# A cross-attention block in one kernel: part of the DMA issues move to ScalarE, epsilon additions may run on GpSimd, and the written-out order is a new one

## The chip, the core and the metric

The kernel runs on one core of a Trainium2 chip. The metric is the device time in microseconds of the whole kernel. A core has TensorE (PE), VectorE (DVE), ScalarE (ACT), GpSimd (POOL) and SyncE (SP), each with an instruction queue of its own that is worked off in order, and 16 DMA engines that all issuers share.

## The reference

All tensors are float32. There are 8 sequences of 256 tokens with 512 channels, 16 heads of 32, and an MLP of width 2048. The mask is all ones.

```
x = layer_norm(hidden) * ln1_w + ln1_b
q = x @ q_w + q_b;  k = ctx @ k_w + k_b;  v = ctx @ v_w + v_b
attn = softmax(q k^T / sqrt(32));  out = (attn v) @ cproj_w + cproj_b
hidden = out + hidden
y = layer_norm(hidden) * ln2_w + ln2_b          # eps = 1e-5 in both
y = gelu_tanh(y @ fc_w + fc_b) @ proj_w + proj_b
return hidden + y
```

## The kernel before

**Groups and stages.** The 8 sequences are worked off in two groups of four (1024 tokens); names carry the group as their first digit. For each group there are the context's and the normalized input's projections (k, v, q), the attention by sequence and four heads at a time (a unit), the output projection `o` with the residual (`hid`), the second normalization (`y`), the `fc` products with gelu (`h`) and the `proj` products (`pd`). The stages of the two groups overlap: group 0's MLP runs beside group 1's attention, group 0's projection beside group 1's output projection, and group 1's MLP comes last.

**Products.** Every large product is a Strassen-Winograd form: seven products of half-size blocks in place of eight, one level for q, k, v and o, two levels in the MLP. The operands' sums and differences (names with `s`, `i` or `t`, such as `pw1s`, `z0i`, `y0t`) are made by VectorE or GpSimd; three PSUM banks X, Y and W take the seven products P1 to P7, and evictions (`take`, `plus` in `quad`) move and add them into the result: t1, t2, t3, c11, c12, c21, c22. ScalarE does part of the plain evictions, VectorE the additions out of PSUM.

**Attention.** `scores` computes a unit's scores, evicts them with the mask's bias on ScalarE (`pr`), takes maxima over blocks on VectorE (`mx`), folds them, writes them to DRAM and loads them back spread over all partitions (`md`, `mm`), subtracts them (`less`, on GpSimd or VectorE) and exponentiates on ScalarE. `attend` multiplies with v and with ones for the sums (`av`); VectorE inverts and scales (`rc`, `r`, `att`).

**The second normalization.** `layer_norm` takes two 128-token tiles at a time. VectorE does statistics and aggregate, adds epsilon, GpSimd raises to −1/2, VectorE makes the bias (`nb`), and ScalarE or VectorE normalizes. For group 0 the tiles are then turned by TensorE (`ps_y`) and evicted with weight and bias to `y`; for group 1 they are stored to DRAM (`yd`), loaded back in pieces of 32x32 (`yb`) and transposed there by VectorE.

**The ends.** `hid` is also stored to DRAM (`hd`). The projection's result is transposed on VectorE (`tr`, into `tq`), the residual is loaded back from `hd` in the same turned layout (`rq`), added (`out`), and stored (`so`). At the very end of group 1 partial results go over DRAM (`lo`, `rl`) and the last quarter by `st`.

**What sets the order.** Nothing is scheduled at run time. The program is built as a list of operations; `Order.run` then replays the table PROGRAM, 2968 words, in its order. A word is an operation's name with the engine's letter behind a colon where the operation has alternatives (V for VectorE, A ScalarE, G GpSimd, S SyncE, P TensorE). A second table, PLACES, gives each buffer its slot. Each engine executes its share in the order of the words, so an instruction that waits holds everything behind it on the same engine. All loads and stores are issued by SP, through `load` and `store`.

Of the kernel before, what the change touches and what calls it, by code (L numbers as in the profile page):

```python
# [17 lines left out]
EPS = 1e-5  # L18
# [111 lines left out]
v0_0_P5 fw0i1_1:G fw0i1_2:G turn_c0_20 v0_0_t3:A fw0i1_3:G turn_c0_30 xt0_5 kws3:V v0_1_t3:A v0_0_P3 fw0i5_2:G rows1  # L130
c0_20:A rows3 stats_x0_10 c0_30:A fw0_01_1 fw0s2:V v0_1_P3 fw1_11_0 v0_0_c12:A xt0_6 fw0s3:V xt0_4 v0_0_P2 fw0i5_4:V
fcd0_7_False fw0i7_3:V fw0i7_1:V xt0_3 c0t4:V fw0i7_2:G fw1_00_1 k0_0_P2 fw0_01_0 stats_x0_01 fw1_10_1 kws1:V
fw0i1_4:G cols v0_1_P2 kws2:V fw0i6_3:G fcd0_1_True cols~1 xt1_0 fcd0_5_False aggr_x0_01 k0_1_P7 fw0i4_3:V k0_1_t1:A
aggr_x0_10 aggr_x0_00 fw0i2_1:G stats_x0_21 k0_0_t1:A fw1_10_0 eps_x0_0 stats_x0_30 pow_x0_0 qw00 k0_1_P2 stats_x0_20
fw1_00_0 fw0i6_1:G aggr_x0_20 nb_x0_0 aggr_x0_21 qw01 fw1i4_3:G fw1i4_1:V k0_0_P6 fw0i2_3:G qw11 stats_x0_11 eps_x0_2
fw1i4_2:V aggr_x0_11 eps_x0_1 fw0i7_4:V k0_1_P6 pow_x0_1 stats_x0_31 k0_0_t2:A norm_x0_01:A k0_1_c11 pow_x0_2
fw0i5_3:V fw0i2_2:G k0_0_P5 v0_1_c11 fcd0_5_True k0_1_t2:A kws4:V fw1i4_4:G k0_0_c11 k0_0_P7 nb_x0_1 v0_0_c11
fcd1_4_True norm_x0_10:A fw0s4:V norm_x0_11:A fcd0_6_False qw10 k0_1_P5 k0_0_t3:A fw1s1:V fcd0_7_True aggr_x0_30
fw1_01_1 fw0i3_3:V k0_0_P3 aggr_x0_31 fw0i3_1:V k0_1_t3:A eps_x0_3 nb_x0_2 fw1i1_1:V pow_x0_3 v0_1_c12:A k0_1_c22
norm_x0_00:A fw1i1_3:G k0_0_c22 k0_1_P3 norm_x0_20:A nb_x0_3 fw0i2_4:V fw1i5_1:G fw1i5_3:V norm_x0_21:A fcd0_2_True  # L140
fw1i1_2:G norm_x0_31:A turn_x0_10 norm_x0_30:V xt1_1 turn_x0_00 fw0i6_2:V k0_1_c12:A fcd0_4_True k0_1_P4 x0_10:A
fw1_01_0 fw0i6_4:V fcd1_5_False k0_0_c12:V x0_00:A fcd0_6_True fw1s3:V turn_x0_31 turn_x0_21 turn_x0_11 fcd0_3_False
fw1i1_4:V x0_21:A k0_0_P4 fw1s2:V x0_11:A fcd1_1_True qws3:V fw1i6_1:G turn_x0_20 fcd1_6_False k0_1_c21 turn_x0_01
fw0i3_2:V fw1i5_2:G q0_1_P1 k0_0_c21 xt1_2 x0_01:A fcd1_7_False x0_20:A fw1i5_4:V qws1:V xt1_3 turn_x0_30 qws2:V
q0_0_P1 x0_30:A x0t1:V x0_31:A x0t2:V q0_0_P2 q0_0_t1:A fw1i6_2:V stats_x1_00 fw1i6_4:G q0_0_P6 cb1_13 q0_0_c11
fw1i2_1:G cb1_02 fw0i3_4:V fw1s4:G stats_x1_01 cb1_10 s000 q0_0_t2:A x0t3:V fcd0_3_True cb1_11 q0_0_P5 ev000_20
ev000_31 fcd1_5_True ev000_21 fw1i2_2:V ev000_01 q0_1_t1:A q0_0_P7 ev000_00 fcd1_3_False x0t4:V ev000_30 fw1i2_4:G
q0_0_t3:A ev000_11 q0_1_P2 mx000_1 ev000_10 fw1i6_3:G aggr_x1_00 q0_0_c22 fcd1_6_True qws4:G q0_1_P6 stats_x1_10
aggr_x1_01 mx000_0 q0_0_P4 fw1i2_3:V mt000 fcd1_2_True q0_1_c11 fw1i3_1:G mc000_2 mc000_1 eps_x1_0 mc000_3 stats_x1_11
cb1_12 fw1i3_2:G q0_1_t2:A q0_0_P3 q0_0_c21 pow_x1_0 aggr_x1_11 fw1i7_1:V fw1i3_4:G fw1i7_2:V s020 fw1i3_3:G  # L150
aggr_x1_10 fold000 q0_1_P5 nb_x1_0 ev020_31 fw1i7_4:G q0_0_c12:V md000 ev020_20 cb1_03 fw1i7_3:G ev020_21 cb1_00
ev020_30 ev020_01 kd0_0_11 mx020_1 s002 ev020_00 cb1_01 ev020_10 ev020_11 fcd1_3_True norm_x1_00:V q0_1_P7 ev002_20
mm000 norm_x1_01:V ev002_10 eps_x1_1 mx020_0 ev002_00 pow_x1_1 ev002_30 ev002_11 v0_0_P7 ev002_31 mt020 q0_1_t3:V
mc020_2 ev002_21 nb_x1_1 q0_1_c22 mc020_3 mc020_1 ev002_01 fold020 s022 mx002_0 md020 v0_1_P7 cb1_30 ev022_21 ev022_01
mx002_1 fcd1_7_True ev022_10 norm_x1_11:A mt002 q0_1_P4 less000_0:G ev022_11 v0_0_c22 mc002_1 mm020 cT1_10
norm_x1_10:A cb1_32 mc002_2 cb1_31 mc002_3 v0_0_P4 ev022_20 fold002 cb1_33 ev022_30 v0_1_c22 less000_1:G ev022_31
md002 ev022_00 q0_1_c21 v0_1_P4 v0_0_c21 cT1_11 exp000_0 less020_0:G s010 cb1_20 v0_1_c21 cb1_23 cT1_01 q0_1_P3
ev010_01 cb1_21 cT1_00 exp000_1 cb1_22 mx022_1 less020_1:G ev010_31 ev010_10 k1_1_P1 mx022_0 ev010_21 mm002 ev010_00
vd0_0_21 ev010_11 mt022 xd1_1 q0_1_c12:V k1_0_P1 mc022_2 c1t1:G ev010_30 mx010_0 vd0_0_11 ev010_20 exp020_0 mx010_1
# [315 lines left out]
def pool(n):  # L475
# [21 lines left out]

SERVE = {
    "cq": 0.72,
    "fw": 0.75, "kw": 0.73, "qw": 0.73, "vw": 0.73, "ow": 0.69, "pw": 0.41, "md": 0.2, "mm": 1.3, "rows": 0.15,  # L500
    "prd0_1_True": 1.36, "res": 1.6, "hid": 1.45,
}
WARM, WARM2 = 14, 14


@with_exitstack
def tile_xattn_block(
    ctx: ExitStack,
    tc: tile.TileContext,
# [23 lines left out]
    nc = tc.nc  # L533
    B, S, D = x.shape
# [949 lines left out]
```

## Time and profile before

| | |
|---|---|
| three runs | 665.8, 673.46, 664.97 us |
| profiled execution, its own time | 665.78 us |
| its span, first to last instruction | 664.0 us |
| TensorE, VectorE, ScalarE, GpSimd busy | 98%, 88%, 52%, 72% |
| bytes moved by DMA | 146.96 MB, 221 GB/s on average |

Busy times are shares of the span. A transfer's issue occupies its engine's queue but isn't counted as busy. In a view of waits a row names who waited, for what, and for how long in total; in a view of groups the number behind the tile's shape is the count, then come the busy time and the mean in ns, then the idle time of the engine ahead of these instructions and what ended it.

### The profile page before, as it was taken

What the parts mean: (1) busy time and instruction counts of PE and PEld (TensorE: products, weight loads), DVE (VectorE), ACT (ScalarE), POOL (GpSimd) and SP (SyncE); (2) the same over time, 40 slices, a digit from 0 to 9 for tenths busy, and PEclk for the clock granted to TensorE, in tenths of its full rate; (3) what the DMA queues carried; (4) which work ended last, traced back from release to release, by engine and by line L of the source; (5) the groups of instructions that cost most, each with busy time, mean ns of one, the idle gap of its engine ahead of it and who ended that gap; (6) DMA issues with size and microseconds to landing.
All of it is one profiled execution on the core that took longest, in us unless ns stands there. A gap on an engine that the chain in (4) does not pass through costs nothing.

```text
span 664.0 us, 11603 instructions
## 1 busy us (share of the span) xinstructions
PE 653.6 (98%) x3985; PEld 493.2 (74%) x3985; DVE 585.3 (88%) x947; ACT 347.6 (52%) x707; POOL 476.4 (72%) x395
## 2 busy tenths in 40 slices
PE   9999999999999999999999999999999999999997
PEld 7845454577545775787777878888888888888887
DVE  3999999989999999999999999988389888898784
ACT  2255687878999789837858993011021123740000
POOL 3764579588869978898899859686366349656670
PEclk9999999999999999999999999999999999999999
DMA  8999898789987675868564466769999998439576
GB/s 269 305 351 341 254 219 270 265 190 214 279 255 215 211 278 187 257 220 267 196 221 144 141 180 202 246 218 277 151 217 230 286 221 229 125 118 223 111 157 114
DMA packets 216539, 146.96 MB, mean 221 GB/s; under 512 B 125424, under 2 KB 176928, under 8 KB 216480
## 3 DMA queue, kind: packets, MB, share of 16 engines
q1 hardware_dynamic: 216480, 146.21, 78.3%
q8 instruction: 32, 0.52, 0.3%
q14 instruction: 27, 0.22, 0.1%
HBM read 105.67 MB, written 40.50 MB: 220 GB/s over the span
## 4 chain that ended last, share of the span: by engine, by line
PE 86%; DVE 7%; ACT 3%; DMA 2%; issue 1%; SPq 0%; POOL 0%; DVEq 0%; POOLq 0%; ACTq 0%
PE pd_X L634 14%; PE fc_X L634 13%; PE pd_W L634 7%; PE av L634 7%; PE fc_W L634 7%; PE v_X L634 4%; PE k_X L634 4%; PE q_X L634 4%; PE s L634 4%; PE fc_Y L634 3%; PE pd_Y L634 3%; PE v_W L634 2%; PE k_W L634 2%; PE q_W L634 2%; PE o_X L634 2%
## 5 line engine op out<-in xcount | busy, mean ns | idle before, releaser
L1029 POOL TENSOR_TENSOR pr<-pr,mm 128x512 f32<-128x512 f32 x82 | 109.4, 1362 | 16.0 <-DMA mm<-md 13.8
L614 ACT ACTIVATE pr<-s,cols 128x256 f32<-128x256 f32 x256 | 104.4, 480 | 20.6 <-PE s L634 16.4
L1004 DVE TRANSPOSE_TENSOR_REDUCE mx<-pr 128x32 f32<-128x1024 f32 x64 | 77.7, 1223 | 3.1 <-ACT pr L614 2.9
L1032 ACT ACTIVATE pr<-pr 128x1024 f32<-128x1024 f32 x64 | 66.9, 1063 | 25.4 <-POOL pr L1029 22.4
L1212 ACT ACTIVATE h<-h,cols 128x256 f32<-128x256 f32 x128 | 56.2, 500 | 45.4 <-DVE h L625 40.2
L625 DVE TENSOR_TENSOR h<-fc_X,h 128x512 f32<-128x512 f32 x80 | 53.4, 680 | 7.8 <-PE fc_X L634 7.4
L634 PE MATMUL av<-pr,ones 128*32 128x256 f32 x512 | 34.8, 383 | 2.4 <-ACT pr L614 1.5
L625 DVE TENSOR_TENSOR h<-fc_W,h 128x512 f32<-128x512 f32 x48 | 31.8, 676 | 3.4 <-PE fc_W L634 2.9
L1024 DVE TENSOR_TENSOR pr<-pr,mm 128x1024 f32<-128x1024 f32 x23 | 32.3, 1415 | 0.0
L623 POOL TENSOR_TENSOR z0i<-z0t,z0i 128x512 f32<-128x512 f32 x14 | 20.9, 1513 | 14.5 <-PE av L634 7.5
L1011 ACT COPY mx<-mx 32x64 f32<-32x64 f32 x96 | 23.3, 243 | 12.7 <-DVE mx L1008 8.3
L634 PEld LDWEIGHTS av<-pr,ones 128*32 128x32 f32 x512 | 14.6, 109 | 18.2 <-ACT pr L614 3.7
L625 POOL TENSOR_TENSOR h<-h,fl 128x512 f32<-128x512 f32 x9 | 11.7, 1315 | 18.5 <-DVE h L625 18.1
L1012 DVE TENSOR_REDUCE mx<-mx 32x32 f32<-32x256 f32 x32 | 18.6, 581 | 3.1 <-ACT mx L1011 3.1
L634 PE MATMUL fc_X<-y1i,fl 128*128 128x256 f32 x80 | 19.7, 379 | 0.0
L625 POOL TENSOR_TENSOR po<-po,e 128x256 f32<-128x256 f32 x10 | 8.9, 910 | 14.0 <-ACT e L606 7.2
L634 PE MATMUL pd_X<-z0i,pl 128*128 128x256 f32 x80 | 18.7, 380 | 0.0
L807 ACT ACTIVATE pl<-hid,rs_y 128x512 f32<-128x512 f32 x1 | 0.8, 813 | 31.7 <-DVE rs_y L799 31.7
L623 POOL TENSOR_TENSOR z0i<-z0t,z0t 128x512 f32<-128x512 f32 x10 | 16.5, 1666 | 1.2 <-DVE z0t L625 1.2
L606 ACT ACTIVATE e<-pd_X,cols 128x256 f32<-128x256 f32 x7 | 3.3, 468 | 26.8 <-PE pd_X L634 26.8
L625 POOL TENSOR_TENSOR tq<-tq,rq 128x512 f32<-128x512 f32 x7 | 9.2, 1320 | 10.9 <-DVE tq L1312 6.3
L634 PEld LDWEIGHTS pd_X<-z0i,pl 128*128 128x128 f32 x80 | 15.1, 190 | 2.4 <-ACT po L601 0.3
(634 smaller groups left out, 1958.0 us busy)
## 6 DMA issues: line engine op xcount, KB each, us to landing
mm<-md SPq DMA_DIRECT2D x32, 512.0 KB, 5.1
pl<-prd SPq DMA_DIRECT2D x55, 256.0 KB, 3.8
fl<-fcd SPq DMA_DIRECT2D x31, 256.0 KB, 4.7
fw<-in_L_xattn_fc_w_dram SPq DMA_DIRECT2D x16, 256.0 KB, 5.8
pw<-in_L_xattn_proj_w_dram SPq DMA_DIRECT2D x32, 128.0 KB, 3.1
hid<-in_x_dram SPq DMA_DIRECT2D x8, 512.0 KB, 7.0
hd<-hid SPq DMA_DIRECT2D x8, 512.0 KB, 5.0
rq<-hd SPq DMA_DIRECT2D x32, 128.0 KB, 5.1
```

The lines of the kernel that those rows point to most:

```text
L606: nc.scalar.activation(to(), of_(), AF.Identity, bias=bias(), scale=1.0)
L614: lambda e: nc.scalar.activation(to(), of_(), AF.Identity, bias=bias(), scale=1.0))
L623: nc.gpsimd.tensor_tensor(to()[:, ts(k, 512)], in0()[:, ts(k, 512)], in1()[:, ts(k, 512)], op)
L625: E[e].tensor_tensor(to(), in0(), in1(), op)
L634: nc.tensor.matmul(o(), l(), r(), start=first, stop=True, skip_group_check=True)
L1004: T.op(f"mx{u}_{h}", [("DVE", 1.126)], [(pr[h], None)], [(mx, [h])], lambda e, h=h: nc.vector.tensor_reduce(tile_of(mx)[:, 0:64].rearrange ...
L1011: lambda e, a=a: nc.scalar.copy(tile_of(mx)[0:32, 64 + 64 * a : 128 + 64 * a], tile_of(mx)[32 * a : 32 * a + 32, 64:128]))
L1012: T.op(f"fold{u}", [("DVE", 0.38)], [(mx, [2, 3, 4, 5])], [(mx, [6])], lambda e: nc.vector.tensor_reduce(tile_of(mx)[0:32, 320:352], tile_ ...
L1024: nc.vector.tensor_tensor(p_, p_, m_[:, :, None, :].to_broadcast([P, 2, 2, S]), ALU.subtract)
L1029: E[e].tensor_tensor(p_, p_, at(M, j)[:, None, :].to_broadcast([P, 2, S]), ALU.subtract)
L1032: lambda e, h=h: nc.scalar.activation(tile_of(pr[h]), tile_of(pr[h]), AF.Exp), table="exp")
L1212: lambda e, f=f, b=b, c=c: nc.scalar.activation(at(h[f][b], c), at(h[f][b], c), AF.Gelu_apprx_tanh, bias=col(c_fcb + f * 4 + c), scale=1.0 ...
```

## The change

First, the transfers of some kinds may be issued by ScalarE as well as by SP: residuals (`rq`), results (`so`, `st`), the y tiles (`yd`, `yb`), `hd`, and the partial results (`lo`, `rl`). The table gives ScalarE 56 of the 136 of these: 17 rq, 18 so, 9 yb, 2 yd, 2 hd, 4 lo, 3 rl and 1 st. Second, the epsilon addition may run on GpSimd: 6 of 16 do, four in the first normalization and two in the second. Third, both tables are new: the same 2968 operations in another order, with other buffer slots (897 of 1290 differ), and some sums, evictions and subtractions on another engine than before. The number of matmuls is the same.

```
+def QUEUES(name):
+    return [("SP", 0.47), ("ACT", 0.47)] if name[:2] in ("rq", "so", "yd", "yb", "hd", "lo", "rl", "st") else [("SP", 0.47)]
...
     def load(name, b, keys, to, of_, mb, src=(), lead=0.0):
         return T.op(
-            name, [("SP", 0.47)], list(src), [(b, keys)],
-            lambda e: nc.sync.dma_start(to(), of_()), serve=served(name, mb), base=2.05, lead=lead,
+            name, QUEUES(name), list(src), [(b, keys)],
+            lambda e: E[e].dma_start(to(), of_()), serve=served(name, mb), base=2.05, lead=lead,
         )
...
-            name, [("SP", 0.47)], src, [(d, keys)] if d else [],
-            lambda e: nc.sync.dma_start(to(), of_()), serve=served(name, mb), base=1.4,
+            name, QUEUES(name), src, [(d, keys)] if d else [],
+            lambda e: E[e].dma_start(to(), of_()), serve=served(name, mb), base=1.4,
...
             def fn1(e, mv=mv, rs=rs):
-                nc.vector.tensor_scalar_add(tile_of(rs)[:, 0:2], tile_of(mv)[:, 1:4:2], EPS)
-            T.op(f"eps_{tag}{g}_{h}", [("DVE", 0.06)], [(mv, None)], [(rs, None)], fn1)
+                E[e].tensor_scalar_add(tile_of(rs)[:, 0:2], tile_of(mv)[:, 1:4:2], EPS)
+            T.op(f"eps_{tag}{g}_{h}", [("DVE", 0.06), ("POOL", 0.2)], [(mv, None)], [(rs, None)], fn1, lock=True)
...
 PROGRAM = """
-cq0_00_0 cq0_00_1 cq0_01_1 cq0_11_0 cq0_11_1 rows8 cq0_01_0 vw00 turn_c0_10 vw11 turn_c0_00 mk small c0_00:A vw10
```

Lines of the changed kernel stand 7 further down than before (L625 becomes L632, L1212 becomes L1219); up to the tables they are 2 to 7 off.

The order moves in every stage. Three places follow. The first is the crossing from attention to the MLP of group 0. VectorE stood thus ahead of the first y tile (`y_00`, which the first fc product reads), with the end of the second normalization (L799 is nb) among scores (`mx`, L1004 to L1012), an inverse (`rc`, `r`) and a subtraction (L1024):

```order
L799 SCALAR_TENSOR_TENSOR rs_y_1_2680<-mv_y_1_2646,rs_y_1_2680 128x2
L1004 TENSOR_REDUCE mx_2682<-pr_1_2585 128x2x2x8
L1008 STREAM_TRANSPOSE mx_2682<-mx_2682 128x64
L799 SCALAR_TENSOR_TENSOR rs_y_0_2692<-mv_y_0_2675,rs_y_0_2692 128x2
L1004 TENSOR_REDUCE mx_2537<-pr_1_2479 128x2x2x8
L1024 TENSOR_TENSOR pr_0_2368<-pr_0_2368,mm_2559 128x1024
L1012 TENSOR_REDUCE mx_2682<-mx_2682 32x32
L1055 TENSOR_REDUCE rc_2785<-av_2703 128x8
L1057 RECIPROCAL rc_2785<-rc_2785 128x8
L1058 STREAM_TRANSPOSE r_2788<-rc_2785 128x256
L1008 STREAM_TRANSPOSE mx_2537<-mx_2537 128x64
L766 TENSOR_SCALAR y_00_2799<-ps_y_00_2758,cols 128x512
```

Now the same engine has this ahead of the same y tile, with a weight sum (`pw1s`) and the scaled attention (`att`) among it:

```order
L806 SCALAR_TENSOR_TENSOR rs_y_0_2720<-mv_y_0_2684,rs_y_0_2720 128x2
L632 TENSOR_TENSOR pw1s_2752<-pw_10_2182,pw_11_2483 128x1024
L796 BN_AGGR mv_y_2_2624<-st_y_2_2604 128x2
L1019 TENSOR_REDUCE mx_2628<-mx_2628 32x32
L800 TENSOR_SCALAR rs_y_2_2780<-mv_y_2_2624 128x2
L1062 TENSOR_REDUCE rc_2785<-av_2733 128x8
L1064 RECIPROCAL rc_2785<-rc_2785 128x8
L1065 STREAM_TRANSPOSE r_2788<-rc_2785 128x256
L1011 TENSOR_REDUCE mx_2722<-pr_0_2475 128x2x2x8
L632 TENSOR_TENSOR att_00_2811<-av_2733,r_2788 128x256
L1015 STREAM_TRANSPOSE mx_2722<-mx_2722 128x64
L773 TENSOR_SCALAR y_00_2836<-ps_y_00_2794,cols 128x512
```

The weight sum, the scaled attention and a later epsilon came in ahead of the y tile, and the subtraction went further forward; over the whole way from the last addition into `hid` to this tile there is also one more maximum (L1011) and one more 256-wide sum (`pw1i`), and one aggregate, one epsilon and one nb fewer.

TensorE had, between the turning of the first tile (`ps_y_00`) and the first fc product, one unit of attention:

```order
L721 MATMUL ps_y_00_2758<-ident,v_1_11_314 128x128
L634 MATMUL av_2767<-pr_0_2273,ones 32x256 x2
...
L634 MATMUL av_2767<-pr_1_2282,xt_0_466 32x256 x2
L634 MATMUL fc_X<-y_00_2799,ow_1913 128x256 x2
L721 MATMUL ps_y_10_2822<-ident,k_1_22_1319 128x128
```

Now two further turnings stand there too, and one more unit (`av_2755`) stands directly ahead of the first turning:

```order
L641 MATMUL av_2755<-pr_1_2278,kw_218 32x256 x2
L728 MATMUL ps_y_00_2794<-ident,xn_y_00_2778 128x128
...
L728 MATMUL ps_y_20_2800<-ident,xn_y_00_2778 128x128
...
L728 MATMUL ps_y_10_2806<-ident,fl_2_2659 128x128
L641 MATMUL av_2819<-pr_0_2362,ones 32x256 x2
...
L641 MATMUL av_2819<-pr_1_2364,v_1_11_1561 32x256 x2
L641 MATMUL fc_X<-y_00_2836,qws_781 128x256 x2
```

Two turnings and a unit moved ahead of the first fc product.

The second place is ScalarE where group 1's second normalization meets the projection of group 0. Before, it held attention tiles (`att`), gelus (L1212), and then norms (L807) and the first y tiles (L751):

```order
L1212 ACTIVATE h_31_3203<-h_31_3203,cols 128x256
L1212 ACTIVATE h_20_3137<-h_20_3137,cols 128x256
L614 ACTIVATE att_10_2979<-att_10_2979,cols 128x512
L614 ACTIVATE att_01_3069<-att_01_3069,cols 128x512
L807 ACTIVATE pl_5_4130<-hid_3_4266,rs_y_3_4423 128x512
L807 ACTIVATE fl_1_3616<-hid_3_4266,rs_y_3_4423 128x512
L807 ACTIVATE xn_y_11_4473<-hid_1_3761,rs_y_1_4458 128x512
```

Now two stores of `hid` stand among the gelus, each with a wait for the last addition into its tile:

```order
L621 ACTIVATE att_11_2958<-att_11_2958,cols 128x512 x2
L601 DMA hd_120<-hid_2_4198 128x2x512
L1219 ACTIVATE h_31_3211<-h_31_3211,cols 128x256
L1219 ACTIVATE h_21_3239<-h_21_3239,cols 128x256
L1219 ACTIVATE h_31_3211<-h_31_3211,cols 128x256
L601 DMA hd_120<-hid_0_4050 128x2x512
L1219 ACTIVATE h_20_3132<-h_20_3132,cols 128x256 x2
L814 ACTIVATE xn_y_30_4433<-hid_3_4264,rs_y_3_4417 128x512
```

Both stores moved from SP's queue into ScalarE's, ahead of three gelus and of two.

The third place is a little later on ScalarE, where the y tiles come back and results go out. Before, there were only these between the norms and the first copies out of the fc banks:

```order
L807 ACTIVATE xn_y_11_4473<-hid_0_4182,rs_y_0_4478 128x512
L606 ACTIVATE e_4548<-pd_X,cols 128x256 x2
L751 ACTIVATE y_00_4683<-y_00_4683,cols 128x512
L606 ACTIVATE e_4548<-pd_X,cols 128x256
L751 ACTIVATE y_01_4696<-y_01_4696,cols 128x512
L601 COPY h_00_4731<-fc_X 128x512
```

Now stores of results (`so`, to out_dram) stand among the evictions of the fc banks:

```order
L758 ACTIVATE y_10_4751<-y_10_4751,cols 128x512 x2
L601 DMA out_dram<-tq_3_4759 32x32x32
L601 DMA out_dram<-tq_1_4710 32x32x32
L1219 ACTIVATE h_00_4767<-h_00_4767,cols 128x256
L601 DMA out_dram<-tq_3_4759 32x32x32 x2
L601 DMA out_dram<-tq_1_4710 32x32x32
L608 COPY e_0_4936<-fc_X 128x512
```

Five stores moved from SP to a place ahead of this copy.

More of the change, by code (lines that the diff above doesn't have):

```diff
@@ L130 @@
[L130 to L159, printed above, removed]
@@ L345 @@
-so1_22 out1_01:V rq1_12 pd12_P4 so1_32 pd12_c12 tr1_01 rl11 tr1_00 so1_20 out1_00:G pd13_P7 rl10 so1_00 pd14_t1
-pd14_P6 pd13_c22 so1_02 pd12_c21 tr1_13 so1_03 so1_33 pd13_P4 pd14_t2 so1_01 tr1_10 tr1_11 out1_10:G pd14_P5 pd13_c21
-tr1_12 out1_11:V pd14_P7 z1i4_4:V so1_11 so1_13 so1_10 pd14_t3 pd14_P2 pd14_P3 pd14_c11 pd14_c22 st00 so1_12 pd14_P4
-pd14_c12 st1 pd14_c21 st01
+cq0_00_1 cq0_00_0 cq0_01_0 cq0_11_0 cq0_01_1 cq0_11_1 vw00 kw00 rows3 fw0_11_1 turn_c0_10 turn_c0_00 c0_10:A vw11
+small c0_00:A vw10 vw01 cq0_10_0 turn_c0_01 rows8 turn_c0_11 c0_01:V turn_c0_31 cq0_10_1 c0_11:V turn_c0_21 fw0_11_0
@@ new lines @@
+v0_0_t3:A stats_x0_20 fw0s4:V xt0_5 v0_0_P3 fw1_10_0 fw1_00_1 kws3:V fw0i3_3:G stats_x0_10 v0_1_P3 v0_0_c12:A qw11
+stats_x0_01 fw0i5_4:G fw1_11_0 aggr_x0_20 v0_0_c11 fw0i2_1:G kws1:V fw0i7_3:G k0_0_P2 v0_1_c12:A aggr_x0_01 aggr_x0_00
+fw0i6_1:V fcd0_1_True eps_x0_0:G kws2:V fw1_10_1 pow_x0_0 k0_0_P7 stats_x0_31 qw10 fcd0_5_True fw0i6_2:G kws4:V
+fcd0_3_False fw0i6_4:G cols k0_1_P2 cols~1 fcd0_6_False stats_x0_11 qw01 k0_0_t1:A aggr_x0_11 k0_1_t1:A stats_x0_30
+k0_1_P7 aggr_x0_31 nb_x0_0 fw0i3_1:V aggr_x0_10 fw1i4_1:V eps_x0_1:G c0t4:V pow_x0_1 k0_0_P6 aggr_x0_30 eps_x0_3:V
@@ new lines @@
+pl15_4=2 pd15_X=C0 po1_2=8 pd15_Y=C3 pd15_W=2 po1_3=36 z1i3_1=82 z1i3_2=16 z1i3_3=64 z1i3_4=40 pl13_1=39 pl13_2=45
+pl13_6=5 pl13_7=66 pl13_5=72 pl13_3=48 pl13_4=42 pd13_X=0 pd13_Y=C3 pd13_W=C0 z1i7_1=38 z1i7_2=48 z1i7_3=88 z1i7_4=6
+pl17_1=63 pl17_2=20 pl17_6=62 pl17_7=50 pl17_5=35 pl17_3=4 pl17_4=34 pd17_X=C1 e1=56 pd17_Y=C2 pd17_W=C4 rq1_2=70
+tq1_2=62 rl0=36 rl1=30 rq1_3=68 tq1_3=0 z1i4_1=34 z1i4_2=20 z1i4_3=32 z1i4_4=18 pl14_1=14 pl14_2=51 pl14_6=50 pl14_7=4
+pl14_5=24 pl14_3=39 pl14_4=77 pd14_X=C1 ot0=61 pd14_Y=C4 pd14_W=1 ot1=1
```

619 lines of the change are left out of this document (322 added, 297 removed).

## The prediction

> **What bounds the kernel now.** I read the head of the page and its chain first, then TensorE's waits, then windows around the largest of them.
>
> ```profile
> span 664.0 us, 11603 instructions
> PE 653.6 (98%) x3985; PEld 493.2 (74%) x3985; DVE 585.3 (88%) x947; ACT 347.6 (52%) x707; POOL 476.4 (72%) x395
> PE 86%; DVE 7%; ACT 3%; DMA 2%; issue 1%; SPq 0%; POOL 0%; DVEq 0%; POOLq 0%; ACTq 0%
> ```
>
> TensorE is busy 653.6 of 664.0 us. What a new order can save while it keeps the 3985 matmuls is the rest, 10.4 us. VectorE is the second limit. The waits tell where those 10.4 us are:
>
> ```profile
> PE av L634 <- ACT pr L614: 1.5, 1, 1.5
> PE first L646 <- DVE warm L641: 1.0, 1, 1.0
> PE av L634 <- ACT pr L1032: 0.8, 1, 0.8
> PE ps_y L721 <- ACT fl L807: 0.8, 1, 0.8
> PE fc_X L634 <- DVE y L766: 0.7, 1, 0.7
> PE fc_W L634 <- DVE h L625: 0.4, 1, 0.4
> PE pd_X L634 <- DVE po L853: 0.3, 1, 0.3
> PE ps_c L721 <- DMA cq<-in_ctx_dram: 0.3, 1, 0.3
> ```
>
> The columns are the total (us), the count and the longest. Only one entry names a transfer, with 0.3 us, and it is a load of the context at the start, a kind that the change leaves on SP. The 1.0 us of `first` lies before any input. At the other end stands the last addition:
>
> ```profile
> 660.61 0.42 DVE L625 TENSOR_TENSOR ot<-pd_W,ot 128x256 f32<-128x256 f32 x1 [1.36 <-PE pd_W L634]
> ```
>
> TensorE ends about there, so about 3.4 us (664.0 less 660.6) are the last addition, the last store and its landing. That leaves 10.4 − 1.0 − 3.4 = **6.0 us** in the middle. Half lies in one place, where group 0 goes from attention and the output projection to its MLP:
>
> ```profile
> 240.00:250.00 10.00, 8.48 (x94) 6.03 (x96) 9.63 (x25) 8.98 (x19) 7.47 (x8) 1.00 0.93 340
> 250.00:260.00 10.00, 8.44 (x109) 5.08 (x98) 8.62 (x17) 9.81 (x22) 9.45 (x10) 1.00 0.66 208
> 400.00:664.00 264.00, 260.27 (x1257) 229.07 (x1255) 215.40 (x338) 50.76 (x106) 163.56 (x122) 1.00 0.80 195
> ```
>
> After the length of the window come the busy times of TensorE, its weight loads, VectorE, ScalarE and GpSimd, then the granted clock (1.00 throughout), the share of the DMA engines and GB/s. The first two windows leave TensorE idle for 1.52 + 1.56 = 3.08 us. From 400 on it is idle for 3.73 us, nearly all of it the 3.4 us of the tail.
>
> **The change, part by part.** All is summed against the profiled execution, 665.78 us, which is the median of the three runs (665.8) to the tenth. Its span is 664.0; about 1.8 us lie around it.
>
> *The second queue.* 56 issues move from SP to ScalarE, nearly all after 400 us. An issue occupies its engine's queue for:
>
> ```profile
> L588 SPq DMA_DIRECT2D yb<-yd x16: 303/560/1798, 460.2 to 482.3; - x16
> L588 SPq DMA_DIRECT2D rq<-hd x32: 318/498/2142, 456.2 to 643.9; - x32
> L594 SPq DMA_DIRECT2D hd<-hid x8: 370/371/807, 238.7 to 449.5; - x8
> ```
>
> At about 0.5 us (the medians) this gives ScalarE 56 × 0.5 = 28 us. It is busy for 50.8 of the 264 us from 400 on (row above), so 213 us are free there and the 28 us lie beside other work. SP loses the same 28 us. What would be gained is a transfer that lands earlier, and no wait of TensorE from 400 on names a transfer: **0** for both. The lower bound is the loss of every middle wait (rival 1), the upper one rival 2. Where ScalarE's issue also has to wait for a store's source, what stands behind it on that engine are gelus and evictions, and behind these TensorE's operands and banks: that is rival 2.
>
> At this place a page speaks against the gain too:
>
> ```profile
> 460.00:480.00 20.00, 19.70 (x91) 17.02 (x91) 9.63 (x17) 0.47 (x1) 9.44 (x8) 1.00 1.19 167
> ```
>
> The share of the DMA engines in these 20 us, where yd, yb and rq run, is 1.19: the engines are full, and a second issuer adds none. The Trainium skill, "DMA: Bandwidth & Descriptors", section "Issuing engines are not separate DMA queues", says that transfers started by several engines run on the same 16 DMA engines, and that a second issuer saves only the time of the issuing. By it the queue's term is 0 as above; by a rule under which two queues doubled the rate it would be 0 as well, since TensorE idles only 0.30 us in that window.
>
> *The epsilon additions.* 6 of 16 go to GpSimd. On VectorE, and the nearest operation on GpSimd (the power that follows, of the same size):
>
> ```profile
> L793 DVE TENSOR_SCALAR rs_x<-mv_x x8: 146/164/175, 34.0 to 120.0; 128x2 f32<-128x2 f32 x8
> L796 POOL TENSOR_TENSOR rs_x<-rs_x,neg_half x8: 683/696/865, 34.2 to 120.3; 128x2 f32<-128x2 f32 x8
> ```
>
> VectorE is relieved of 6 × 0.16 = 1.0 us. The chain of one normalization grows by between 0 (as short as on VectorE) and 0.70 − 0.16 = 0.5 us; I take 0.5, as the nearest row. It is hidden where the normalized tile waits for other tiles of the group; uncovered it costs 0.5 once, in the crossing below. Term: 0.
>
> *The order: the crossing at 240 to 260.* The chain runs from the last addition into hid (o_0's W product) through statistics, epsilon, power, norm and turn to the first y tile, which the first fc product reads:
>
> ```profile
> 243.84 0.69 DVE L625 TENSOR_TENSOR hid<-o_W,hid 128x512 f32<-128x512 f32 x1
> 256.62 0.77 DVE L766 TENSOR_SCALAR y<-ps_y,cols 128x512 f32<-128x512 f32 x1
> 257.45 1.13 PE L634 MATMUL fc_X<-y,ow 128*128 128x256 f32 x4 [0.66 <-DVE y L766]
> 258.76 1.77 DVE L625 TENSOR_TENSOR pw1s<-pw,pw 128x1024 f32<-128x1024 f32 x1
> 259.99 1.07 PE L634 MATMUL av<-pr,ones 128*32 128x256 f32 x16
> 261.86 0.48 PE L634 MATMUL fc_Y<-y,ow 128*128 128x256 f32 x1
> ...
> 265.73 0.33 PE L721 MATMUL ps_y<-ident,k 128*128 128x128 f32 x1
> 266.22 0.60 PE L634 MATMUL fc_X<-y0i,fl 128*128 128x256 f32 x2
> ```
>
> The y tile starts 12.78 us after the hid addition starts. In the new order VectorE has other rows between the same two: one maximum of scores more, one 1024-wide weight sum (1.77 us, the row at 258.76), one 256-wide sum, one product of attention with the inverse, and one aggregate, one epsilon (now on GpSimd) and one nb row less.
>
> ```profile
> L1004 DVE TRANSPOSE_TENSOR_REDUCE mx<-pr 128x32 f32<-128x1024 f32 x64 | 77.7, 1223 | 3.1 <-ACT pr L614 2.9
> L625 DVE TENSOR_TENSOR att<-av,r 128x256 f32<-128x256 f32 x32 | 12.6, 405 | 0.2
> L625 DVE TENSOR_TENSOR fw0i<-fw0s 128x256 f32<-128x256 f32 x6 | 2.9, 492 | 0.0
> L793 DVE TENSOR_SCALAR rs_y<-mv_y 128x2 f32<-128x2 f32 x8 | 2.7, 366 | 0.8 <-ACT fl L807 0.8
> L799 DVE SCALAR_TENSOR_TENSOR rs_y<-mv_y,rs_y 128x2 f32<-128x2 f32 x8 | 2.5, 324 | 0.9 <-POOL rs_y L796 0.9
> L789 DVE BATCH_NORM_AGGREGATE mv_y<-st_y 128x2 f32<-128x6 f32 x16 | 2.3, 165 | 0.1
> ```
>
> 1.22 + 1.77 + 0.49 + 0.41 − 0.17 − 0.37 − 0.32 = 3.03 us more, if VectorE idles there as before; it idled 20 − 9.63 − 8.62 = 1.75 us in the two windows, and if the added rows fill that, y is late by 1.28 only. Against it TensorE gets work ahead of the first fc product: one more av unit (259.99 to 261.86, 1.87) and two more turns (265.73 to 266.22, 0.49 each), 2.85 us. The difference lies between 1.28 − 2.85 = −1.57 and 3.03 − 2.85 = +0.18; I take the middle, **−0.7**, which is about the 0.66 us that the first fc product waits now. What is late next is the norm behind the powers: GpSimd now does one epsilon and two powers ahead of the needed one where it did two powers, which is within the +0.5 above.
>
> *The start.* The 4x128 load of bias rows that stood ahead of a piece of the first context quarters stands behind them now; the 0.3 us of `ps_c` go: **−0.3**.
>
> *The rest of the order.* All other middle waits are 6.0 − 0.7 − 0.3 = 5.0 us. Rows are exchanged everywhere, with engines too; by my tally of the rows at their durations VectorE gets about 7.6 us more and GpSimd about 9 us less, an estimate. I take these waits as neither removed nor added, since a shuffled order of the same work on a VectorE that is busy for 91% of the two windows above gives others like them; bounds −5.0 and the same +5.0. The tail keeps its last product, addition and store: 0.
>
> **Sum: 665.78 − 0.7 − 0.3 = 664.8 us.**
>
> **The rivals.**
> 1. *The order closes the middle waits.* 665.78 − 6.0 = **659.8**, and a little less where TensorE loses small steps between rows that the view does not list. For it: half of the idle is at one crossing, which has 2.85 us more of work to cover it. Against it: VectorE gets rows there, and the longest waits (av on `pr`, 1.5 and 0.8) hang on the scores' chain over ScalarE and GpSimd, which no row shows shortened.
> 2. *ScalarE's queue holds what TensorE waits for: slower.* One place is the second store of hid, whose source is VectorE's last addition of its sequence pair; behind it on ScalarE now stand two gelus, which the projection's next product needs.
>
> ```profile
> 434.57 1.67 PE L634 MATMUL o_W<-fl,a1t 128*128 128x256 f32 x7
> 438.41 0.68 DVE L625 TENSOR_TENSOR hid<-o_W,hid 128x512 f32<-128x512 f32 x1
> 439.11 0.37 SPq L594 DMA_DIRECT2D hd<-hid  x1
> L1212 ACT ACTIVATE h<-h,cols 128x256 f32<-128x256 f32 x70 | 30.1, 498 | 44.2 <-DVE h L625 40.2 <-POOL h L625 4.0
> ```
>
> The product's eight matmuls end at about 436.5 and the addition at 439.1, 2.6 us later; with the issue (0.37) and two gelus (2 × 0.50) the operand is there 4.0 us after the product, and TensorE has 6.9 us of other products ahead of the reader, by the order. It decides when VectorE is over 2.9 us later than now at that addition. By my tally its rows there grow by up to 6.7 us, which would be a wait of 3.8: 668.6. A second place of the same kind are five stores of results ahead of the eviction of an fc bank that TensorE asks for about a product (1.89 us) later: 5 × 0.49 + 0.58 for the eviction − 1.89 = +1.1. Both: **669.7**. Beyond 2%, over 679.1, it would need about four such places at once; most are covered by ScalarE's idle 213 us.
> 3. *The queues share turns.* The weights on SP get their turn against ScalarE's transfers of many small pieces.
>
> ```profile
> fl<-fcd SPq DMA_DIRECT2D x31, 256.0 KB, 4.7
> ```
>
> If a weight block that lands in 4.7 us now takes twice that once where the fc products begin, and nothing covers it, that is 664.8 + 4.7 = **669.5**. Against it: the blocks are loaded some products ahead. The Trainium skill, on the same page, section "Queues, rings and completion order", has each DMA engine take turns between its queues packet by packet, which is the mechanism of this rival; no row here shows two queues of data (the page of before lists one, and two of instructions).
>
> **How the numbers follow.** Forecast 0.52, rival 1 0.21, rival 2 0.19, rival 3 0.08. The range runs from 659.0 (rival 1, with the small steps) to 671.0 (rivals 2 and 3 with one further issue of the slow kind, 1.80 in the row of yb, less the cover). What is left out is half of rival 2's tail and the unforeseen, under 0.2. A change of 2%, 13.3 us, is about what a measurement of this kernel can tell from no change. Faster than that, below 652.5, would take more than all that TensorE idles in the middle: 0.01. Slower: a quarter of rival 2's chance, where the places add: 0.05. Within 2%: 0.94.
>
> **What would show it.** Right: TensorE busy for about 653.6 us, waits that sum to about 5 in the middle, the fc_X wait on y gone, ScalarE with about 28 us of issuing and no TensorE wait behind it, landing times of fl near 4.7, no wait on a transfer after 400. Wrong towards rival 1: two windows around the crossing with TensorE near 10. Towards rival 2: waits of pd_X on gelus (h) or of fc products on ScalarE's evictions after 400. Towards rival 3: waits on fl or pl. I would be wrong altogether if TensorE's busy time itself moved.

## The result, and the profile after

| | before | changed |
|---|---|---|
| median of 20 runs each | 665.47 us | 672.04 us (668.98 to 675.19) |
| ratio, 95% interval | | 1.0088 (1.0067 to 1.0109) |
| profiled execution, its span | 665.78, 664.0 us | 671.07, 669.2 us |

The changed kernel is slower by 0.9%, about 5.9 us by the ratio and 6.6 us by the medians. That is less than 2% but clear of noise, and the median lies 1.0 us above the range that was given. A ratio also takes in runs with a granted clock below 0.999, which for the kernel before are about 6 us longer and make up 8 of its 31, 13 of its 34 and none of its 23 runs beside the three rounds of experiments below, so the medians stand beside the ratios. The head of the page of the changed kernel:

```profile
span 669.2 us, 11633 instructions
PE 652.7 (98%) x3985; PEld 494.4 (74%) x3985; DVE 581.3 (87%) x953; ACT 348.4 (52%) x705; POOL 452.4 (68%) x390
q1 hardware_dynamic: 168736, 138.21, 71.0%
q10 hardware_dynamic: 47744, 8.00, 7.6%
PE 68%; DVE 10%; DMA 8%; issue 5%; ACT 4%; POOL 4%; SPq 1%; ACTq 0%; POOLq 0%; DVEq 0%
```

TensorE's work is the same (652.7 us against 653.6). The second queue is there: q10 with 8.00 MB. In the chain DMA has grown from 2% to 8% and "issue" from 1% to 5%, at TensorE's expense (86% to 68%). The windows by stage say where it happened; the first four rows are of before, the other four of the changed kernel (length, then busy time of TensorE, weight loads, VectorE, ScalarE, GpSimd):

```profile
0.00:180.00 180.00, 178.74 (x1117) 109.28 (x1118) 158.17 (x272) 118.45 (x244) 122.47 (x115) 1.00 0.90 269
180.00:280.00 100.00, 95.78 (x789) 61.85 (x787) 96.61 (x164) 87.61 (x181) 87.00 (x72) 1.00 0.74 235
280.00:440.00 160.00, 158.80 (x1014) 128.07 (x1011) 154.04 (x230) 95.66 (x188) 137.86 (x108) 1.00 0.63 200
440.00:640.00 200.00, 199.70 (x927) 174.73 (x926) 163.32 (x258) 45.87 (x96) 122.27 (x98) 1.00 0.84 199
```

```profile
0.00:180.00 180.00, 178.35 (x1116) 108.89 (x1117) 155.85 (x272) 116.98 (x242) 117.12 (x118) 1.00 0.91 267
180.00:280.00 100.00, 95.92 (x806) 63.96 (x804) 96.72 (x166) 88.54 (x180) 86.94 (x70) 1.00 0.74 233
280.00:440.00 160.00, 158.28 (x1009) 129.16 (x1002) 152.20 (x239) 99.32 (x191) 116.17 (x101) 1.00 0.67 216
440.00:640.00 200.00, 194.40 (x900) 168.59 (x899) 158.32 (x243) 43.52 (x93) 117.20 (x94) 1.00 0.84 191
```

TensorE's idle time rises from 1.26 to 1.65, from 4.22 to 4.08, from 1.20 to 1.72, and from **0.30 to 5.60 us**. All but 0.8 us of the loss lies behind 440 us, where nearly all of the moved transfers are. The tail is the same to 0.1 us. TensorE's waits, the largest of the changed kernel:

```profile
PE av L641 <- ACT pr L621: 3.1, 2, 2.0
PE fc_X L641 <- ACT e L608: 2.0, 1, 2.0
PE pd_W L641 <- DVE e L632: 1.8, 2, 1.5
PE fc_W L641 <- DMA e<-fcd: 1.4, 1, 1.4
PE av L641 <- ACT pr L1039: 1.2, 1, 1.2
PE first L653 <- DVE warm L648: 1.0, 1, 1.0
```

The second, third and fourth are new and lie behind 440 us (of the third, 0.9 us stay when the queue is undone, experiment 1). The second is the place that the prediction named, five stores ahead of the copy of an fc bank. ScalarE's timeline there:

```profile
508.58 0.51 ACT L1219 ACTIVATE h<-h,cols 128x256 f32<-128x256 f32 x1 [4.63 <-DVE h L632]
508.59 5.84 ACTq L601 DMA_DIRECT2D out_dram<-tq  x3
514.48 0.59 ACT L608 COPY e<-fc_X 128x512 f32<-128x512 f32 x1 [5.38 <-DMA out_dram<-tq]
```

Three stores take 5.84 us of ScalarE's queue, and the copy behind them has a 5.38 us gap that "DMA out_dram<-tq" ends: the landing of a store. The operands of the single issues in the trace tell why. Each transfer signals its landing on a semaphore; the program has eight for all its 612 transfers (101 and 103 to 109 in the operands, 76 or 77 transfers each), given out in turn in program order whatever queue issues them: in the kernel before, SP's issues take them strictly in this turn, and in the changed kernel the issues of both queues, put together, fit one such turn. A transfer whose semaphore is still taken waits at its issue until the transfer eight places before in the program has landed:

```
start    engine  transfer         waits for, signals   landed
506.96   ScalarE out_dram<-tq     107, 107             512.30
512.32   ScalarE out_dram<-tq     107, 107             516.68
560.92   ScalarE out_dram<-tq     109, 109             566.34
566.36   SP      fl<-prd          109, 109             571.63
```

The second store starts 0.02 us behind the landing of the first. The last two rows show the same wait from one queue to the other: a weight load on SP waits for a store that ScalarE issued, and `e<-fcd`, for which TensorE waits 1.4 us at 570.6, stands next behind it on SP. So the theory under test, A (A1 in its sharper form): the two queues are coupled through eight semaphores, and each holds what stands behind it on its engine. The other theories, B to D, are named in the expectations.

### The profile page after: what moved, and what is told of

Same layout as the page of the kernel before. It is cut to its first block, busy times and chain, and to the rows that moved or that the text cites. A ratio compares the mean times of both kernels' runs of the same rounds, so it can differ in the third digit from the quotient of the medians.

```text
span 669.2 us, 11633 instructions
## 1 busy us (share of the span) xinstructions
PE 652.7 (98%) x3985; PEld 494.4 (74%) x3985; DVE 581.3 (87%) x953; ACT 348.4 (52%) x705; POOL 452.4 (68%) x390
## 4 chain that ended last, share of the span: by engine, by line
PE 68%; DVE 10%; DMA 8%; issue 5%; ACT 4%; POOL 4%; SPq 1%; ACTq 0%; POOLq 0%; DVEq 0%
PE fc_X L641 11%; PE pd_X L641 10%; PE fc_W L641 6%; PE pd_W L641 6%; PE av L641 5%; PE k_X L641 4%; PE o_X L641 3%; PE v_X L641 3%; PE s L641 3%; PE pd_Y L641 2%; PE fc_Y L641 2%; PE q_X L641 2%; PE k_W L641 2%; PE o_W L641 2%; ACT pr L621 2%
## 5 line engine op out<-in xcount | busy, mean ns | idle before, releaser
L1036 POOL TENSOR_TENSOR pr<-pr,mm 128x512 f32<-128x512 f32 x78 | 101.0, 1324 | 20.5 <-DMA mm<-md 16.0
L1219 ACT ACTIVATE h<-h,cols 128x256 f32<-128x256 f32 x128 | 56.2, 500 | 68.1 <-DVE h L632 26.6
L1011 DVE TRANSPOSE_TENSOR_REDUCE mx<-pr 128x32 f32<-128x1024 f32 x64 | 77.0, 1219 | 2.6 <-ACT pr L621 2.4
L632 DVE TENSOR_TENSOR h<-fc_X,h 128x512 f32<-128x512 f32 x80 | 53.2, 679 | 10.8 <-PE fc_X L641 10.3
L632 DVE TENSOR_TENSOR h<-fc_W,h 128x512 f32<-128x512 f32 x48 | 32.3, 679 | 6.4 <-PE fc_W L641 5.8
L632 POOL TENSOR_TENSOR h<-h,fl 128x512 f32<-128x512 f32 x8 | 11.6, 1454 | 16.1 <-DVE h L632 16.1
L641 PE MATMUL pd_W<-z0i,pl 128*128 128x256 f32 x80 | 18.9, 381 | 1.8 <-DVE e L632 1.5
L613 ACT ACTIVATE e<-pd_X,cols 128x256 f32<-128x256 f32 x4 | 1.9, 474 | 33.8 <-PE pd_X L641 33.8
L630 POOL TENSOR_TENSOR z0i<-h,h 128x512 f32<-128x512 f32 x8 | 12.1, 1528 | 10.9 <-DVE po L632 10.2
L641 PEld LDWEIGHTS pd_W<-z0i,pl 128*128 128x128 f32 x80 | 15.0, 190 | 4.5 <-issue 2.6
L632 DVE TENSOR_TENSOR h<-fc_Y,h 128x512 f32<-128x512 f32 x24 | 16.3, 678 | 2.0 <-PE fc_Y L641 1.9
L632 POOL TENSOR_TENSOR tq<-tq,rq 128x512 f32<-128x512 f32 x8 | 10.8, 1354 | 9.8 <-DVE tq L1319 9.6
L630 POOL TENSOR_TENSOR z0t<-h,h 128x512 f32<-128x512 f32 x10 | 14.6, 1474 | 4.2 <-issue 4.2
L630 POOL TENSOR_TENSOR z1t<-h,z1t 128x512 f32<-128x512 f32 x6 | 9.6, 1612 | 11.6 <-PE pd_X L641 11.6
L630 POOL TENSOR_TENSOR z1i<-h,h 128x512 f32<-128x512 f32 x8 | 11.3, 1440 | 7.7 <-PE pd_X L641 7.7
```

The source lines that it names most:

```text
L613: nc.scalar.activation(to(), of_(), AF.Identity, bias=bias(), scale=1.0)
L630: nc.gpsimd.tensor_tensor(to()[:, ts(k, 512)], in0()[:, ts(k, 512)], in1()[:, ts(k, 512)], op)
L632: E[e].tensor_tensor(to(), in0(), in1(), op)
L641: nc.tensor.matmul(o(), l(), r(), start=first, stop=True, skip_group_check=True)
L1011: T.op(f"mx{u}_{h}", [("DVE", 1.126)], [(pr[h], None)], [(mx, [h])], lambda e, h=h: nc.vector.tensor_reduce(tile_of(mx)[:, 0:64].rearrange ...
L1036: E[e].tensor_tensor(p_, p_, at(M, j)[:, None, :].to_broadcast([P, 2, S]), ALU.subtract)
```

## The experiments

All were run beside the kernel before on the same chip (7, 9 and 11 on another chip than the others); ratios are to that, and where it matters its median stands beside.

**1. The queue undone.** Each of the 56 words gets S. (Transfers of these kinds are 111 in the table, 55 of them on SP already; the 136 given ahead is wrong.)

```
-... hd6:A ... so0_33:A ... rq1_03:A ... st1:A
+... hd6:S ... so0_33:S ... rq1_03:S ... st1:S
```

> The changed kernel with all 56 transfers issued by SP again, order, engines and slots otherwise as changed. Theory A (the second queue costs: ScalarE's issues wait for landings and hold its evictions, and SP's weight loads wait for transfers that ScalarE issues late): the wait of an fc product on ScalarE's copy (2.0 us) and the one on a weight load (1.4 us) go, 672.0 - 3.4 = about 668.6. Theory B (the new order of VectorE, GpSimd and ScalarE costs, the queue does not): 672.0 within 1. Theory C (the queue helped and hides a worse order): SP's queue gets late and the time rises, 674 or more.

Measured: 666.66 us, ratio 0.9992 (0.9965 to 1.0020). By the ratio the whole loss is gone; by the medians 5.4 us of 6.6 are, more than the two named waits, and 1.2 us stay (666.66 beside 665.43). By stages:

```profile
180.00:280.00 100.00, 95.23 (x794) 63.41 (x792) 97.04 (x164) 88.50 (x180) 86.00 (x70) 1.00 0.71 228
280.00:440.00 160.00, 158.30 (x1014) 129.18 (x1014) 151.56 (x239) 99.10 (x191) 117.54 (x101) 1.00 0.65 216
440.00:640.00 200.00, 197.84 (x920) 172.39 (x919) 161.95 (x249) 43.43 (x93) 123.73 (x96) 1.00 0.82 193
```

Behind 440 the idle time falls from 5.60 to 2.16 us, 3.4 us, which is the difference of the two profiled spans (669.2 and 665.8); ahead of it nothing gets better. The medians differ by 5.4, since either profiled execution lies about 1 us from its kernel's median (671.07 and 672.04, 667.71 and 666.66). Theories B and C fall.

**2. The queue alone.** The order of before, with the same 56 words on ScalarE.

```
-so0_33 ... rq1_03 ... st1
+so0_33:A ... rq1_03:A ... st1:A
```

> The kernel before, its order, engines and slots, with the same 56 transfers issued by ScalarE at the places where SP issued them. Theory A: ScalarE's evictions are held here too, 2 to 5 us slower than before: 667.5 to 670.5. Theory B: 665.5 within 1. Theory C: 1 to 3 us faster than before.

Measured: 666.51 us, ratio 0.9997 (0.9963 to 1.0031): no cost that can be told from none. That contradicts A as I had put it: the issues themselves, with all their queue time, cost nothing in the old order. Its idle time behind 440 is 0.29 us:

```profile
440.00:640.00 200.00, 199.71 (x925) 174.66 (x924) 163.57 (x257) 46.06 (x96) 122.56 (x98) 1.00 0.90 199
```

Here too SP waited for ScalarE's transfers (3.65 us at 609, 4.32 us at 616, by starts and semaphores in the trace), but what stood behind was not needed yet. The loss belongs to the queue and the new order together.

**3. Epsilon undone.**

```
-eps_x0_0:G eps_x0_1:G eps_x1_0:G eps_x1_1:G eps_y0_3:G eps_y1_3:G
+eps_x0_0:V eps_x0_1:V eps_x1_0:V eps_x1_1:V eps_y0_3:V eps_y1_3:V
```

> The changed kernel with the 6 epsilon additions on VectorE again. All theories: 672.0 within 1.5, since 6 x 0.16 us on VectorE against at most 0.5 us on a chain stands beside other work. If the epsilon on GpSimd were what delays the crossing into fc0, 1 us or more faster.

Measured: 671.79 us, ratio 1.0076 (1.0044 to 1.0109). No difference from the changed kernel (672.04 us, 1.0088) clear of noise.

**4. The five stores behind the copy,** still on ScalarE.

```
-so0_33:A fc101_P4 fl105_0 so0_11:A ... so0_30:A fc111_c21 so0_32:A ... so0_10:A ... fc117_t1:A
+fc101_P4 fl105_0 ... fc111_c21 ... fc117_t1:A so0_33:A so0_11:A so0_30:A so0_32:A so0_10:A
```

> The changed kernel with the five stores of results that stand on ScalarE ahead of the copy of an fc bank moved directly behind that copy, still on ScalarE. Theory A: the 2.0 us wait of the fc product on this copy goes, about 670.0, or less of a gain if the stores hold the next copies instead. Theory B: the wait stays and the time too, 672.0 within 1.

Measured: 673.97 us, ratio 1.0094 (1.0060 to 1.0129): no gain. The wait went from this copy to the next one:

```profile
PE fc_X L641 <- ACT fl L608: 2.9, 1, 2.9
PE fc_W L641 <- DMA e<-fcd: 1.8, 1, 1.8
```

```profile
517.30 0.33 SPq L595 DMA_DIRECT2D pl<-in_L_xattn_fc_w_dram  x1
514.69 6.97 ACTq L601 DMA_DIRECT2D out_dram<-tq  x3
521.75 0.59 ACT L608 COPY fl<-fc_X 128x512 f32<-128x512 f32 x1 [8.55 <-DMA fl<-in_L_xattn_fc_w_dram]
```

SP's weight load at 517.30 starts 0.01 us after a ScalarE store of 512.67 has landed (517.29), 5.76 us after SP's issue before it had ended; and one of the three ScalarE stores starts at 519.59, when that weight load has landed (519.57). Each queue waits for the other in turn.

**5. The result stores alone on SP** (19 words).

```
-so0_12:A ... so1_10:A ... st1:A
+so0_12:S ... so1_10:S ... st1:S
```

> The changed kernel with the 19 result stores (so, st) issued by SP again; residuals, y pieces and the rest stay on ScalarE. Theory A1 (a result store holds ScalarE's evictions while it waits for the landing of the transfer that used its semaphore eight transfers before, and SP's weight loads wait for the late ScalarE stores in the same way): most of the 5.4 us come back, 668.5, the waits on the copy e (2.0) and on the weight load (1.4) are gone. Theory A2 (what costs are the residual and y loads on ScalarE): 671 to 672, the waits stay.

Measured: 670.21 us, ratio 1.0046 (1.0007 to 1.0084). By the medians 1.8 of the 6.6 us come back, by the ratios about half: less than expected. The wait on the copy e is gone, but the one on the weight load stays at 1.4 us:

```profile
PE fc_W L641 <- DMA e<-fcd: 1.4, 1, 1.4
```

**6. The residual and y loads alone on SP** (26 words).

```
-yb1_01:A ... rq0_22:A ... rq1_32:A
+yb1_01:S ... rq0_22:S ... rq1_32:S
```

> The changed kernel with the 26 loads of residuals and y pieces (rq, yb) issued by SP again; the result stores stay on ScalarE. A1: 671, only the wait of 1.5 us on VectorE's addition at 459 may go; the wait on the copy e stays near 2. A2: 667 to 668.

Measured: 673.08 us, ratio 1.0097 (1.0061 to 1.0133): no gain, and neither theory's wait. The wait on the copy e is gone here too, and a new one is larger than any before:

```profile
PE fc_Y L641 <- DMA fl<-in_L_xattn_fc_w_dram: 3.8, 1, 3.8
```

SP's and ScalarE's queues ahead of it:

```profile
489.02 0.42 SPq L595 DMA_DIRECT2D pl<-in_L_xattn_fc_w_dram  x1
495.15 0.38 ACTq L601 DMA_DIRECT2D out_dram<-tq  x1
497.50 0.32 SPq L595 DMA_DIRECT2D fl<-fcd  x1
```

SP issues nothing for 8.05 us. Its load at 497.50 waits for semaphore 107, whose last transfer is the ScalarE store of 495.15, landed at 497.48. ScalarE came to that store late, since its result was not ready (VectorE's addition into `tq` ended at 495.07); the weights behind SP's load were late for it.

**7. As 6, with that one store on SP.**

```
-so0_12:A
+so0_12:S
```

> The kernel with residual and y loads on SP and the result stores on ScalarE, with one of these stores (the first on ScalarE, so0_12) moved to SP. There SP stood still from 489.4 to 497.5 us ahead of a weight load that uses the semaphore of this store, which ScalarE issued at 495.2 and which landed at 497.5; a product then waited 3.8 us for weights. Theory A1 (SP's issue waits for the landing of the late ScalarE store eight transfers before): the 3.8 us wait goes, 673.1 - 3.8 = 669.3. Theory D (SP was simply behind, with full DMA engines): the wait stays, 672 to 673.

Measured: 672.3 us, ratio 1.0123 (1.0104 to 1.0142). The wait at 503 went as foretold, and the time did not:

```profile
PE fc_W L641 <- DMA fl<-in_L_xattn_fc_w_dram: 4.2, 1, 4.2
```

```profile
500.43 0.34 SPq L601 DMA_DIRECT2D out_dram<-tq  x1
509.06 1.00 ACTq L601 DMA_DIRECT2D out_dram<-tq  x2
511.58 0.33 SPq L595 DMA_DIRECT2D fl<-in_L_xattn_fc_w_dram  x1
```

Now SP stands for 10.81 us, from 500.77 to 511.58, at a load with semaphore 105, last used by the next ScalarE store, that of 509.06. A1 foresaw the wait but not its successor. D falls, though the time is the one that it gave: SP issued nothing at all in those 10.81 us, and the DMA engines were far from full (share 0.40, next to last in the first line below).

In 4, 6 and 7 the time holds more than these waits. The windows around the longest wait, the first two of run 7 and the last of run 6, show a lower granted clock (third from the end):

```profile
500.00:510.00 10.00, 10.00 (x47) 8.64 (x47) 7.16 (x14) 3.08 (x5) 5.54 (x6) 1.00 0.40 87
510.00:520.00 10.00, 5.85 (x19) 4.53 (x19) 4.48 (x8) 0.52 (x2) 2.89 (x5) 0.83 0.95 210
500.00:510.00 10.00, 6.21 (x23) 4.80 (x22) 3.86 (x7) 3.01 (x5) 2.93 (x3) 0.85 1.05 232
```

It is also 0.91 from 520 to 540 us in 4, and from 240 to 260 us in all three. TensorE is busy for 655.4, 655.8 and 657.1 us in them against 652.7 in the changed kernel's profile, where the same windows show 1.00. So "no gain" there is true of the time and not of the waits alone: in 6 TensorE idles 4.54 us behind 440, less than the 5.60 of the changed kernel. That a long wait brings the lower clock on is not shown: from 240 to 260 us the changed kernel idles longer (2.76 us) than 6 (1.96).

**8. Only the five stores on SP.**

```
-so0_33:A so0_11:A so0_30:A so0_32:A so0_10:A
+so0_33:S so0_11:S so0_30:S so0_32:S so0_10:S
```

> The changed kernel with only the five result stores ahead of the copy e issued by SP, at their places in the order. A1: the hold of ScalarE ahead of e (5.4 us) and the 2.0 us wait of the fc product go, and nothing takes their place, 670.0, unlike where the five were moved behind the copy. If any order near this one costs as much, 672.

Measured: 670.38 us, ratio 1.0053 (1.0020 to 1.0087), 1.7 us of the 6.6 by the medians. The wait on the copy e is gone. The size is near the forecast, though waits of the same kind grew elsewhere, one on another ScalarE copy:

```profile
PE fc_X L641 <- ACT h L608: 1.9, 1, 1.9
```

**9. Stores and loads on SP** (45 words), 11 of the 56 still on ScalarE.

```
-... yb1_01:A ... rq0_22:A ... so0_12:A ... st1:A
+... yb1_01:S ... rq0_22:S ... so0_12:S ... st1:S
```

> The changed kernel with result stores, residual loads and y loads all on SP (45 of the 56); only 2 hid stores, 2 yd stores and the partial results stay on ScalarE. A1: the coupling between the two queues is gone from 455 to 630, and the whole loss comes back: 666.7 within 1.5, though stores alone gave 670.2 and loads alone 673.1. If the remaining 11 cost: 668 or more.

Measured: 666.3 us, ratio 1.0020 (1.0003 to 1.0036). Nearly all of it comes back, as A1 has it: with one of the two kinds left on ScalarE (5, 6) most of the loss stays, or all of it. Idle behind 440 is 0.86 us:

```profile
440.00:640.00 200.00, 199.14 (x927) 173.94 (x926) 163.49 (x250) 43.43 (x93) 125.50 (x98) 1.00 0.82 192
```

The coupling can be summed from the traces: the time that ScalarE's issues stand waiting for their own semaphore, and SP's for one that ScalarE used last. It is 42.2 us in the changed kernel, 52.8 in 4, 35.2 in 5, 17.7 in 6, 22.3 in 7, 41.7 in 8, and 0 in 1 and 9. It is also 36.6 us in 2, where nothing is lost, so the sum doesn't give the time: what stands behind each wait does.

**10. A wait of the order taken away,** on top of 1.

```
-z0t2_1:V gelu0_311 ox00 gelu0_333 gelu0_210 less113_0:V gelu0_302 pd03_P1 gelu0_303 gelu0_120 less113_1:V
+less113_1:V less113_0:V z0t2_1:V gelu0_311 ox00 gelu0_333 gelu0_210 gelu0_302 pd03_P1 gelu0_303 gelu0_120
```

> All 56 transfers on SP, and on VectorE the two subtractions of the last but one unit of attention moved ahead of a 1024-wide sum, the one that the first exponential needs first. The wait of 1.15 us of av on the exponential at 390 goes: 666.7 - 1.1 = 665.5. If VectorE's later sums are then late, the wait comes back at a projection product and it stays at 666.7.

Measured: 665.69 us, ratio 0.9964 (0.9929 to 1.0000); the wait of av on the exponential fell from 1.15 to 0.10 us. Its median is the lowest here, but by the medians (665.69 beside 666.04) the gain over the kernel before is 0.05%, and the interval of the ratio reaches 1.0000: a gain over before isn't shown.

**11. Another one,** on top of 10.

```
-ev132_01 ev132_11 ev132_10 stats_y0_00 less120_1:G pw1_01_10 ev101_10 ... ev101_11
+ev132_01 ev132_11 ev101_10 ev101_11 ev132_10 stats_y0_00 less120_1:G pw1_01_10 ...
```

> All transfers on SP, the subtractions first as before, and on ScalarE two evictions of scores, those that free the bank of the next av product, moved ahead of two others. The wait of av on the eviction (1.96 us at 246) falls to about 0.9: 665.7 - 1.1 = 664.6, against 665.5 to 666.0 of the kernel before. If the next unit then waits for its bank instead, 665.7.

Measured: 666.35 us, ratio 1.0017 (1.0007 to 1.0028). The wait did shrink:

```profile
PE av L641 <- ACT pr L621: 2.5, 3, 1.1
PE ps_y L728 <- ACT xn_y L814: 0.9, 1, 0.9
```

Its largest single one is 1.1 us now instead of 2.0, but two others come in (0.38 us on the next unit, and 0.9 us of the turning on the norm, 0.3 in 10). No gain is shown: the medians of 10 and 11 differ by 0.7 us, on two chips, and beside each the kernel before has a median of its own (666.04 and 665.36).

## Why the prediction was wrong

- **The failed step is the second queue's term.** It put 0 and gave as cover that 28 us of issuing fit into ScalarE's 213 free us. That argues from the duration of an issue. What holds ScalarE is the wait in front of it: in the changed kernel ScalarE's 56 issues stood waiting for their own semaphore for 31.3 us, 24.3 of them for a transfer that SP had issued, and SP's for 10.9 us on semaphores last used by ScalarE (summed from starts, landings and operands in the trace). Put at 0, the term measured +5.4 us in this order (experiment 1, by the medians), 3.4 us of it visible in the profiled runs.
- **"SP loses the same 28 us" was no relief either.** SP's weight loads now wait for transfers that ScalarE reaches late. The sentence that no TensorE wait from 400 on names a transfer was true of before, and was used as if it held for any order.
- **Rival 2 had the right place and half of the mechanism.** The five stores held the copy of the fc bank, for 2.0 us where it had 1.1; the store of hid held ScalarE for 3.9 us and no one waited. It put the price on the issue instead of the landing, and did not see that SP is held in turn, so its sum of 669.7 was 2.3 us short of the median and the upper bound of 671.0, made of it, 1.0 us.
- **Rival 3's price did not come, but its sharing isn't excluded.** The weights did not land later: fl from fcd took 4.0 us (4.7 before; medians). The transfers that ScalarE issued did land later, yb in 7.3 us and rq in 6.6 (5.3 and 5.1 before), and a later landing holds its semaphore longer. No run here parts the two.
- **The rest of the order: 0 within 5.0 held.** With the queue undone, the new order gives 666.66 us beside 665.43 (ratio 0.9992). The working behind it did not hold: by the tally VectorE was to get about 7.6 us more and GpSimd 9 us less, and the pages show 4.0 less (585.3 to 581.3) and 24.0 less (476.4 to 452.4).
- **The crossing's −0.7 came near by number and not in effect.** Idle from 240 to 280 fell from 3.78 to 2.76 us (windows of 20 us; 3.46 with the queue undone), and the wait of the first fc product on y is gone. The y tile follows the hid addition by 13.23 us (12.78 before), only 0.45 later instead of 1.28 to 3.03:

```profile
245.43 0.69 DVE L632 TENSOR_TENSOR hid<-o_W,hid 128x512 f32<-128x512 f32 x1
258.66 0.77 DVE L773 TENSOR_SCALAR y<-ps_y,cols 128x512 f32<-128x512 f32 x1
```

But TensorE waits longer for an eviction of scores just ahead, first before and then changed:

```profile
247.21 1.07 PE L634 MATMUL av<-pr,ones 128*32 128x256 f32 x16 [1.47 <-ACT pr L614]
249.29 1.07 PE L641 MATMUL av<-pr,ones 128*32 128x256 f32 x16 [1.96 <-ACT pr L621]
```

Over the whole stage, 180 to 280, it idles 4.08 us against 4.22, and 4.77 with the queue undone, so the nearness of the number is luck. The start's −0.3 did not come; `ps_c` still waits 0.3 us for the context.

- **Epsilon at 0** holds (experiment 3).
- The page cited ahead, the Trainium skill, "DMA: Bandwidth & Descriptors", section "Issuing engines are not separate DMA queues", says that a second issuer saves only issuing time. Experiment 2 agrees that nothing is gained (0.9997); that it can lose is seen here beside it (experiment 1 against the changed kernel). The prediction's reading that a share of 1.19 means full engines was wrong, though: the same 20 us show 1.41 in the changed kernel, while the rate moved only from 167 to 184 GB/s.

What wasn't tried: to give each queue landing semaphores of its own, so the number of eight itself was never varied. That the waits follow it rests on the operands and on starts that fall within 0.02 us of landings (the rows of issues above, experiments 4, 6 and 7), on the coupling being 0 where the time comes back (1, 9), and on 7, which moved the wait to the next such store. Which part of the new order makes the coupling cost stays open too.

## What to carry to other kernels

An issue that moves to another engine takes along its waits, also those that only appear at run time: before a second queue is credited with free time, look up which semaphore each transfer signals and which earlier landing it must wait for. Where both queues share these in program order, a store whose data comes late on one engine stops the loads of the other; it looks safer to put only transfers on the second queue whose data is ready when their turn comes, which no run here tried, or none. Moving one offender need not help while the next stands behind it (7); even a whole kind gave little (5) or nothing (6), and both kinds together nearly all (9).

## What was not expected of the hardware

A DMA issue whose own row shows 0.33 us stood at SP for 10.81 us (experiment 7) while the page's busy times show nothing of it, since issuing and waiting there are not counted. In the changed kernel's chain it shows only as a larger share of "issue" and DMA (1% to 5%, 2% to 8%). In the kernel before, SP's issues wait for their own semaphore too, 7.1 us in all, and no wait of TensorE from 400 on names a transfer.
